# Four small moves in the self-attention stage of a decoder block: sixteen products of ones at the start, one load on another queue, the first snapshot earlier among the exponentials, and a third output tile begun before the last pair

## The chip, the cores and the metric

The kernel runs on one core of a Trainium2 chip. The metric is the time of one execution on the device, in microseconds (us); lower is better. Three executions of the kernel before took 1611.61, 1611.78 and 1612.36 us, so their median is 1611.78 us.

A core has five engines with an instruction stream each: the matrix engine (PE in the profile, with its weight loads as PEld), the vector engine (DVE), the scalar engine (ACT), the general engine (POOL) and the sync engine (SP), which here only issues DMA transfers. They wait for each other through semaphores.

## The reference

Inputs are x (8 batches of 224 rows, 512 columns) and a context (8 of 750 rows, 384 columns), all in 32-bit floats. The block has three parts, each followed by a residual add and a layernorm. Only the first is touched:

```python
x = _rmsnorm(tokens, norm_w)
q = x @ Wq;  k, v = split(x @ Wkv)          # 16 heads of 64
q, k = _head_rmsnorm(q, q_gamma), _head_rmsnorm(k, k_gamma)
sim = tanh(q k^T / 50) * 50 * 64**-0.5
out = softmax(sim) @ v
x = layernorm(tokens + out.reshape(...) @ Wo)
```

After it come a cross-attention against the context (with Wq, Wk, Wv, Wo and a bias) and a feed-forward part with ternary weights and 8-bit activations.

## The kernel before

**Tiling and turns.** The 8·224 = 1792 rows are 14 tiles of 128 rows, and four groups g of two batches (448 rows, `G`). The 16 heads are 8 pairs hp. The self-attention stage runs 32 turns, m = 8g + hp: one head pair of one group each (loop at L758). A turn is a software pipeline over three head pairs: it multiplies the weights of pair m-1 with the values (`self_values`, L632), makes the scores of pair m (`self_scores`, L559), and makes q and k of pair m+2 (`products_qk`, L475). In most turns one tile of v (`project_v`, L539) or one finished tile of the output projection (`self_output`, L661) follows. The order on each engine is the order in which this code is written; no scheduler changes it.

**Scores and exponentials.** `self_scores` issues the score products of both batches u into two PSUM tiles (`sc_a`) and returns a list of eight scalar-engine calls (L585): for u = 0 tanh of 128 rows, tanh of 96 rows, exp of 128 rows, exp of 96 rows, then the same for u = 1. They all have line L282 in the profile (L772 in the last two turns) and write `pr`.

**Seven products instead of eight.** `half_products` (L274) makes q and k of two batches by a Strassen-like scheme: seven half-size products over three PSUM accumulators x_, z_ and w_ (`q_x`, `q_z`, `q_w` at L470; each product is two matmuls of 224 columns, which the profile shows as four instructions). The accumulator x_ is used four times in a row without being cleared. Between two uses the scalar engine takes a snapshot of it: m1 after the first product (L296, tile `qm`), u2 after the second (L304, `qu`), u4 after the third (L312, `qu`). The next product into x_ has to wait until the snapshot is taken. The order of the products is x_, z_, x_ (+s2·t2), w_, x_ (+s1·t1), w_, x_ (+s4·b22).

The eight calls of the exponentials are popped between these instructions by `filling(n)`. Their order on the scalar engine before the change is: three calls, m1, three calls, u2, one call, the copy c22 (L309), one call, u4 (L312), c11 (L315), and later c12 (L328). The snapshots m1 and u2 lie among the exponentials in the same queue, so both the calls ahead of a snapshot and the product that it reads decide when it is taken.

**What else the scalar engine does in a turn.** It squares q and k (L499), which waits for a vector-engine add (L324); it moves v from PSUM to its place (L554), in as many pieces as the tile has runs of rows that may go with one instruction, one to four, of about 0.68 us each; and it squares a tile of x (L371). The eight calls of the next turn stand behind all that.

**Start and end.** `first_loads` (L105) issues the first loads on SP: a tile of transposed x, the norm weights, 128 columns of Wq (`load_cols(0, 0, P)`, L108), three more tiles of transposed x, and so on. `weigh_x` (L393) multiplies a tile by the norm weights on the vector engine, and `block_qk` (L405) makes q of the first pair from it, tile by tile. At the end (L855 to L863) two of the last four tiles get the output products of the first seven pairs, then the values of the last pair are made and scaled on the vector engine (`weigh`, L649), POOL copies the rows that straddle two groups (`oT_joint`, L659), and then the two tiles get their last pair and the other two tiles all eight pairs.

The matmul accumulators of 128 x 512 come from a pool of three (`a_mm`), the score tiles from a pool of two (`a_sc`, which also gives w_), and the tile of the weighted values from a pool of one (`a_ov`).

Of the kernel before, what the change touches and what calls it, by code (L numbers as in the profile page):

```python
# [21 lines left out]
F32 = mybir.dt.float32  # L22
# [17 lines left out]
P = 128  # L40
# [6 lines left out]
NPAIR = HEADS // 2  # L47
# [18 lines left out]
def decoder_block(ctx: ExitStack, tc: tile.TileContext, a: dict, out: bass.AP):  # L66
    nc = tc.nc
# [11 lines left out]
    def load_x(i):  # L79
        nc.sync.dma_start(out=x[i], in_=x_in[i * P : (i + 1) * P, :])  # L80
# [7 lines left out]

    ws = [wpool.tile([P, KD, INNER], F32, tag="w", name=n) for n in ("wq", "wk", "wv")]

    def load_cols(j, c0, c1):

        name, at = (("attn_Wq", 0), ("attn_Wkv", 0), ("attn_Wkv", INNER))[j]
        src = a[name].rearrange("(k p) n -> p k n", p=P)
        nc.sync.dma_start(out=ws[j][:, :, c0:c1], in_=src[:, :, at + c0 : at + c1])

    norm_w = const.tile([P, KD, 1], F32, name="norm_w")
    gam = const.tile([P, 2, NPAIR, 1], F32, name="gam")
# [3 lines left out]
    def load_xT(y, i):  # L102
        nc.sync.dma_start(out=y, in_=xT_in[:, :, i * P : (i + 1) * P])

    def first_loads(xnT):  # L105
        load_xT(xnT[:, :, :P], 0)
        nc.sync.dma_start(out=norm_w[:, :, 0], in_=a["norm_w"])
        load_cols(0, 0, P)  # L108
        for i in range(1, 4):
            load_xT(xnT[:, :, i * P : (i + 1) * P], i)  # L110
        load_cols(1, 0, P)
        load_cols(2, 0, 512)
        for i in range(4):
            load_x(i)
        nc.sync.dma_start(out=gam[:, 0, :, 0], in_=a["q_gamma"])
        nc.sync.dma_start(out=gam[:, 1, :, 0], in_=a["k_gamma"])
        for cols in ((P, 2 * P), (2 * P, INNER)):
            for j in range(2):
                load_cols(j, *cols)
        for i in range(4, NX // 2):  # L120
            load_x(i)
        load_cols(2, 512, INNER)
        for i in range(NX // 2, NX):
            load_x(i)
# [68 lines left out]
    ones = const.tile([P, P], F32, name="ones")  # L193
# [35 lines left out]
    def pieces(i):  # L229

        at = i * P
        while at < (i + 1) * P:
            b = at // S
            n = min((i + 1) * P, (b + 1) * S) - at
            yield b, at - b * S, at - i * P, n
            at += n
# [7 lines left out]
    def key_pieces(i):  # L244

        for b, c, at, n in pieces(i):
            while n:
                kt = c // P  # L250
                row = c % P
                m = min([n, P - row] + [64 if s == 64 else 32 for s in (row, at) if s])
                yield b, kt, row, at, m
                c, at, n = c + m, at + m, n - m
# [16 lines left out]

    def half_products(product, a, b, sums_a, sums_b, dest, parts, acc, third=None, fill=None):  # L274

        def filling(n):  # L280
            for _ in range(n if fill else 0):
                fill.pop(0)()  # L282

        between = bool(fill)
        (a11, a12), (_, a22) = a
        (b11, _), (b21, b22) = b
        s1, s2, s3, s4 = sums_a
        t1, t2, t3, t4n = sums_b
        c11, c12, c21, c22 = (dest(r, c) for r in range(2) for c in range(2))
        m1, u2, u4 = parts  # L290
        x_, z_, w_ = acc
        if third:
            a13, a23, b31, b32, dif = third
        filling(3)
        product(x_, a11, b11, True)
        nc.scalar.copy(m1, x_)  # L296
        filling(3)
        product(z_, a12, b21, True)
        if third:
            product(z_, a13, b31, False)  # L300
        if not between:
            nc.scalar.copy(c11, z_)
        product(x_, s2, t2, False)
        nc.scalar.copy(u2, x_)  # L304
        filling(1)
        product(w_, s3, t3, True)
        if third:
            product(w_, a23, b32, False)
        nc.scalar.copy(c22, w_)  # L309
        filling(1)  # L310
        product(x_, s1, t1, False)
        nc.scalar.copy(u4, x_)  # L312
        if between:
            nc.gpsimd.tensor_tensor(c22, c22, u4, ALU.add)
            nc.scalar.copy(c11, z_)  # L315
            nc.gpsimd.tensor_tensor(c11, c11, m1, ALU.add)
        else:
            nc.gpsimd.tensor_tensor(c11, c11, m1, ALU.add)
            nc.gpsimd.tensor_tensor(c22, c22, u4, ALU.add)
        yield  # L320
        product(w_, a22, t4n, False)
        if third:
            product(w_, a23, dif, False)
        nc.vector.tensor_tensor(c21, w_, u2, ALU.add)  # L324
        product(x_, s4, b22, False)
        if third:
            product(x_, a13, b32, False)
        nc.scalar.copy(c12, x_)  # L328
        yield
# [6 lines left out]
    NG = B // 2  # L336
# [6 lines left out]
    opened = [range(first[g], first[g + 1]) for g in range(NG)]  # L343

    with tc.tile_pool(name="a_sb", bufs=2) as sb, tc.tile_pool(
        name="a_mm", bufs=3, space=PSUM
    ) as ps_mm, tc.tile_pool(name="a_sc", bufs=2, space=PSUM) as ps_sc, tc.tile_pool(
        name="a_ov", bufs=1, space=PSUM
# [119 lines left out]
        def product_qk(mm, c, w, start):  # L468
            for k in range(2):
# [2 lines left out]
                    skip_group_check=True,  # L472
                )

        def products_qk(m, calls):  # L475
            g, hp = divmod(m, NPAIR)
            qk[m] = sb.tile([P, 2, G], F32, name="qk", bufs=3)
            x_, z_ = (ps_mm.tile([P, S], F32, tag="mm", name=f"q_{n}") for n in "xz")
            w_ = ps_sc.tile([P, 2, 512], F32, tag="sc", name="q_w")[:, 0, :S]
            if m < NPAIR + 2:  # L480
                q, k = ([w[:, 2 * kh : 2 * kh + 2, hp * P : (hp + 1) * P] for kh in range(2)]
                    for w in (wq, wk))
                b = (q[0], None), (q[1], k[1])
                t = [work[:, hp % 4, i] for i in range(4)]
            else:
                w7 = stream[:, m % 2]
                b = (w7[:, 0], None), (w7[:, 1], w7[:, 2])
                t = [w7[:, 3 + i] for i in range(4)]
            return half_products(
                product_qk, input_blocks(g), b, [sums_x[:, i] for i in range(4)], t,  # L490
                lambda u, w: qk[m][:, w, u * S : (u + 1) * S],
                [sb.tile([P, S], F32, name=n, bufs=1) for n in ("qm1", "qu2", "qu4")],
                [x_, z_, w_],
                fill=calls,
            )

        def square_qk(m):
# [163 lines left out]
        def self_output(g, i, hp0=0, hp1=NPAIR):  # L661

            if hp0 == 0:
                outs[i] = ps_mm.tile([P, DIM], F32, tag="mm", name="mm_o")
            mm = outs[i]
            at = i * P - g * G
            for hp in range(hp0, hp1):
                o = oT[g * NPAIR + hp].rearrange("p u q -> p (u q)")
                nc.tensor.matmul(  # L669
                    mm,  # L670
                    lhsT=joint[g][:, hp, :] if at < 0 else o[:, at : at + P],
                    rhs=wo[:, hp, :],
                    start=(hp == 0),
                    stop=(hp == NPAIR - 1),
                )
            if hp1 < NPAIR:
                return
            nc.vector.tensor_tensor(x[i], mm, x[i], ALU.add)
            due.append(i)
# [48 lines left out]
            nc.sync.dma_start(out=wq7[:, 3:], in_=sums_xq[:, g])  # L728

        joint, outs, due, scales, ovs = {}, {}, [], [], {}  # L730

        for i in range(4):
            weigh_x(i)
            block_qk(0, 0, (i * P, min((i + 1) * P, G)))
# [19 lines left out]
        for i in opened[0][2:]:  # L754
            project_v(i, 0)

        out_at = [(), (2, 3, 5), (0, 2, 4, 6), (3, 5, 6)]
        for m in range(NS):  # L758
            g, hp = divmod(m, NPAIR)
            ahead = opened[g + 1] if g + 1 < NG else ()  # L760
# [38 lines left out]
            tiles = opened[g + hp // 4] if g + hp // 4 < NG else ()  # L799
# [55 lines left out]
        last = closed[NG - 1]  # L855
# [1 line left out]
            self_output(NG - 1, i, 0, NPAIR - 1)  # L857
        self_values(NS - 1)
        weigh(NS - 1)
        for i in last[:2]:  # L860
            self_output(NG - 1, i, NPAIR - 1)
        for i in last[2:]:
            self_output(NG - 1, i)  # L863

        for f in [layernorm([i]) for i in due]:
# [7 lines left out]
    parts = const.tile([P, 3, NCHUNK], F32, name="w_parts")  # L873
# [56 lines left out]
    with tc.tile_pool(name="c_sb", bufs=1, reuse_waits="tile") as sb, tc.tile_pool(  # L930
        name="c_mm", bufs=7, space=PSUM, reuse_waits="tile"
    ) as ps_mm, tc.tile_pool(
        name="c_nm", bufs=1, space=PSUM, reuse_waits="tile"
# [466 lines left out]
        for t, i0, i1 in ((18, 0, 7), (26, 7, LATE)):  # L1400
            job(t, roots, i0, i1)
            n = t + 1
# [9 lines left out]
        for i in range(NX):  # L1412
            b = ((i + 1) * P - 1) // S
# [9 lines left out]
        for t in range(-1, TURNS):  # L1423
# [19 lines left out]
            fill = []  # L1443
            if t == TURNS - 1:
                fill = [
                    partial(cross_project, i, k, k + 2)
                    for i in done[t] for k in range(0, NPAIR - 2, 2)
                ]
# [52 lines left out]
            if t % (2 * QG) >= 2 * QG - 2 and t > 0 and t + 2 < TURNS:  # L1501
                b = 2 * (t // (2 * QG) + 1) + t % 2
# [13 lines left out]
        last = done[TURNS]  # L1516
# [12 lines left out]
    with tc.tile_pool(name="f_sb", bufs=2, reuse_waits="tile") as sb, tc.tile_pool(  # L1529
        name="f_mm", bufs=6, space=PSUM, reuse_waits="tile"  # L1530
    ) as ps_mm, tc.tile_pool(
        name="f_dn", bufs=2, space=PSUM, reuse_waits="tile"
# [215 lines left out]
```

## Time and profile before

| what | value |
|---|---|
| median of three executions | 1611.78 us |
| the profiled execution: its time, its span | 1611.31 us, 1609.5 us |
| PE busy | 1588.8 us (99% of the span) |
| PEld busy | 1138.0 us (71%) |
| DVE busy | 1326.7 us (82%) |
| ACT busy | 996.8 us (62%) |
| POOL busy | 961.8 us (60%) |
| self-attention | from 0 to about 492 us |

The span is from the first to the last instruction of the program. A busy time counts the stretches in which an engine had an instruction at work; waiting, branching and DMA issuing are not counted. The busy time of PE is that of pipelined matmuls with modelled ends, so neighbours overlap a little: the distance between the starts of two neighbours is the better measure of what a product costs. In a timeline line stand the start in us from the beginning of the span, the length, the engine, the line of the source, what it writes and reads, the shape, and how many instructions were merged; in brackets the idle time of the engine before it and what ended it.

### The profile page before, as it was taken

Reading aid. Unit: us, or ns where it says so; the run is one execution under the profiler, and the core shown is the slowest. Engines: PE = TensorE matmul, PEld = TensorE weight load, DVE = VectorE, ACT = ScalarE, POOL = GpSimd, SP = SyncE. Lnnn points to the kernel's source line nnn. Section 1 sums busy time; section 2 is a strip of 40 time slices with the busy share of each in tenths; the row PEclk is TensorE's granted clock in tenths of the full one; section 3 lists DMA queues with packets and bytes.
Section 4 is the critical chain, followed back from the end, with each engine's and each line's share of the span. In section 5 each row is a group of like instructions: output and inputs, shape, how many; then the busy total and the mean of one; then the engine's idle time right before and its main releaser. Section 6 shows DMA issues by size and latency. Waiting matters only on the chain.

```text
span 1609.5 us, 27132 instructions
## 1 busy us (share of the span) xinstructions
PE 1588.8 (99%) x9668; PEld 1138.0 (71%) x9682; DVE 1326.7 (82%) x2813; ACT 996.8 (62%) x1858; POOL 961.8 (60%) x887
## 2 busy tenths in 40 slices
PE   8999999999999999999999999999999999999998
PEld 5767666667747888876887876788876888764443
DVE  3999897889976798886798886798887898978877
ACT  5667555656525677764667775687764666635663
POOL 5785575666524757685465685457686566752244
PEclk9999999999999999999999999999999999999999
DMA  8115242433204313241122252223240111214343
GB/s 300 47 53 196 81 133 89 138 89 118 82 20 161 104 56 103 65 154 57 60 66 80 78 187 63 72 77 121 78 161 24 34 44 39 75 46 92 66 92 105
DMA packets 143111, 149.14 MB, mean 93 GB/s; under 512 B 41088, under 2 KB 109184, under 8 KB 142592
## 3 DMA queue, kind: packets, MB, share of 16 engines
q1 hardware_dynamic: 142976, 147.40, 30.0%
q8 instruction: 77, 1.26, 0.3%
q14 instruction: 58, 0.48, 0.1%
HBM read 119.85 MB, written 18.87 MB: 86 GB/s over the span
## 4 chain that ended last, share of the span: by engine, by line
PE 85%; DVE 9%; ACT 2%; issue 2%; DMA 1%; POOL 0%; SPq 0%; POOLq 0%; DVEq 0%; ACTq 0%
PE sc_c L1244 9%; PE ov_c L1374 8%; PE v_x L1075 6%; PE mm_co L262 6%; PE mm_f L1547 6%; PE k_x L1069 5%; PE mm_v L544 5%; PE q_x L470 5%; PE v_w L1075 5%; PE k_w L1069 4%; PE mm_o L669 4%; PE mq_x L1082 3%; PE v_z L1075 2%; PE q_w L470 2%; PE sc_a L571 2%; PE ov_a L640 2%
## 5 line engine op out<-in xcount | busy, mean ns | idle before, releaser
L1361 POOL TENSOR_TENSOR csh<-cpT 125x672 f32<-125x672 f32 x128 | 210.0, 1640 | 111.0 <-DVE cpT L1346 94.3
L200 POOL TENSOR_TENSOR nm_i<-nm_q,mhalf 128x28 f32<-128x28 f32 x32 | 157.9, 4935 | 81.8 <-DVE nm_q L519 81.4
L1346 DVE TENSOR_TENSOR cpT<-cpT,mx_b 125x1344 f32<-125x1344 f32 x128 | 192.6, 1545 | 2.8
L1226 ACT COPY cpT<-sc_c 125x448 f32<-125x448 f32 x384 | 173.5, 570 | 17.6 <-PE sc_c L1244 10.6
L1358 ACT ACTIVATE cpT<-cpT 125x1344 f32<-125x1344 f32 x128 | 168.4, 1328 | 11.4 <-DVE cpT L1346 11.2
L1244 PE MATMUL sc_c<-cq,ckT 64*125 64x224 f32 x1536 | 164.2, 359 | 3.4 <-ACT cpT L1226 1.7
L1244 PEld LDWEIGHTS sc_c<-cq,ckT 64*125 64x125 f32 x1536 | 147.7, 183 | 19.1 <-issue 10.3
L1374 PE MATMUL ov_c<-cpT,cv 125*64 125x224 f32 x1536 | 152.9, 355 | 0.2 <-ACT cpT L1358 0.2
L1106 POOL TENSOR_TENSOR cv<-cv,cvmu 125x384 f32<-125x384 f32 x32 | 31.9, 997 | 195.3 <-ACT cv L1105 195.3
L1374 PEld LDWEIGHTS ov_c<-cpT,cv 125*64 125x64 f32 x1536 | 107.6, 137 | 44.6 <-issue 8.8
L544 PE MATMUL mm_v<-wv,xnT 128*128 128x512 f32 x224 | 100.4, 592 | 0.0
L1547 PE MATMUL mm_f<-ternary,xqT 128*128 128x512 bf16 x435 | 98.0, 379 | 1.5 <-DVE h L1557 0.8
L262 PE MATMUL mm_co<-xattn_Wo,coT 128*128 128x512 f32 x224 | 98.5, 593 | 0.0
L1230 DVE TENSOR_TENSOR xw<-sc_c,cpT 125x448 f32<-125x448 f32 x64 | 39.7, 620 | 67.6 <-PE sc_c L1244 59.0
L282 ACT ACTIVATE pr<-sc_a 128x448 f32<-128x448 f32 x120 | 57.9, 535 | 60.4 <-PE sc_a L571 60.2
L1362 POOL TENSOR_TENSOR csm<-csh 125x224 f32<-125x224 f32 x128 | 85.0, 664 | 10.0
L1363 POOL TENSOR_TENSOR csm<-csm,csh 125x224 f32<-125x224 f32 x128 | 84.5, 660 | 10.0
L595 DVE TRANSPOSE_TENSOR_REDUCE sm_q<-pr 128x28 f32<-128x896 f32 x64 | 70.7, 1104 | 19.3 <-ACT pr L282 18.9
L1254 ACT COPY ov_s<-ov_c 128x448 f32<-128x448 f32 x31 | 16.5, 531 | 110.7 <-PE ov_c L1374 110.7
L669 PE MATMUL mm_o<-attn_Wo,oT 128*128 128x512 f32 x192 | 84.3, 593 | 0.0
L1547 PEld LDWEIGHTS <-xqT 128*128 128x128 bf16 x448 | 43.8, 98 | 54.2 <-issue 1.7
L554 ACT ACTIVATE v<-mm_v,rms_rs 32x512 f32<-32x512 f32 (+2 forms) x80 | 54.4, 680 | 36.7 <-PE mm_v L544 35.9
(239 smaller groups left out, 3967.1 us busy)
## 6 DMA issues: line engine op xcount, KB each, us to landing
w_slot<-qk_sums SPq DMA_DIRECT2D x22, 512.0 KB, 3.6
xw<-w_sums SPq DMA_DIRECT2D x32, 320.0 KB, 2.9
xwq<-xq_sums SPq DMA_DIRECT2D x16, 512.0 KB, 4.2
w_stage<-w_gateT SPq DMA_DIRECT2D x16, 512.0 KB, 5.4
w_stage<-w_upT SPq DMA_DIRECT2D x16, 512.0 KB, 4.9
w_stage<-w_downT SPq DMA_DIRECT2D x16, 512.0 KB, 4.5
tern<-w_t SPq DMA_DIRECT2D x24, 256.0 KB, 2.7
ternary<-tern SPq DMA_DIRECT2D x3, 2048.0 KB, 7.8
```

The source lines that it names most:

```text
L200: nc.gpsimd.tensor_tensor(y, v, mhalf.to_broadcast([P, v.shape[-1]]), ALU.pow)
L262: nc.tensor.matmul(mm, lhsT=oT[:, k, c : c + P], rhs=w[:, k, :], start=(k == 0), stop=(k == NPAIR - 1),)
L544: nc.tensor.matmul(mm, lhsT=xnT[:, k, at : at + P], rhs=wv[:, k, c * 512 : (c + 1) * 512], start=(k == 0), stop=(k == KD - 1),)
L669: nc.tensor.matmul(mm, lhsT=joint[g][:, hp, :] if at < 0 else o[:, at : at + P], rhs=wo[:, hp, :], start=(hp == 0), stop=(hp == NPAIR - 1),)
L1075: nc.tensor.matmul(mm[:, t, :], lhsT=c[:, t * CT : (t + 1) * CT], rhs=w, start=start and t == 0, stop=True, skip_group_check=True,)
L1226: nc.scalar.copy(pT[:, j, 2 * c2 : 2 * c2 + 2, :], banks[c2][j])
L1244: nc.tensor.matmul(sc[j][:, i, :], lhsT=kT[h0 : h0 + DH, w, ct * CT : (ct + 1) * CT], rhs=cq[h0 : h0 + DH, t % 2, w], start=True, stop=True,)
L1346: nc.vector.tensor_tensor(pT[:, j], pT[:, j], nm[:CT, j] .rearrange("p (o q) -> p o q", o=1) .to_broadcast([CT, NCT, S]), ALU.add,)
L1358: nc.scalar.activation(pT[:, j], pT[:, j], AF.Exp)
L1361: nc.gpsimd.tensor_tensor(half, pT[:, j, 0:3], pT[:, j, 3:6], ALU.add)
L1374: nc.tensor.matmul(ov[h0 : h0 + DH, w, :], lhsT=v[:, ct, hq * DH : (hq + 1) * DH], rhs=pTs[w][:, j, ct, :], start=(ct == 0), stop=(ct == N ...
L1547: nc.tensor.matmul(mm, lhsT=xqTs[i][:, k, :], rhs=w[:, k, cols], start=(k == 0), stop=(k == KD - 1),)
```

## The change

Four edits, all in the self-attention stage:

1. Ahead of the first `weigh_x`, PE gets 16 matmuls of a 128 x 128 tile of ones with itself, into the tile `ov_a`. Nothing reads the result, and the tile's next user overwrites it. They wait only for POOL's memset of the ones (L194).
2. The first 128 columns of Wq are issued from the scalar engine's queue, where they are the first instruction after the entry barrier, ahead of the load of the activation tables. They were third on SP's queue.
3. `half_products` pops `ahead` calls before m1 and 6 - `ahead` between m1 and u2, in place of three and three. `products_qk` passes 0 in the turns that `crowded` names and 2 in the others. `crowded(m)` holds in turn 0, and where the v tile of turn m-1 has four or more pieces and that turn had no output tile. Worked out, it holds in turns 0, 3, 6, 7, 10, 15, 22, 26 and 27; the products are made in turns 0 to 29, so 21 turns have `ahead=2`.
4. At the end the third of the four last tiles gets its first seven pairs after the last values and their scaling are issued, and before the last pair of the first two tiles.

```diff
-    def load_cols(j, c0, c1):
+    def load_cols(j, c0, c1, queue=nc.sync):
...
-        nc.sync.dma_start(out=ws[j][:, :, c0:c1], in_=src[:, :, at + c0 : at + c1])
+        queue.dma_start(out=ws[j][:, :, c0:c1], in_=src[:, :, at + c0 : at + c1])
...
-        load_cols(0, 0, P)
+        load_cols(0, 0, P, nc.scalar)
...
-        filling(3)
+        filling(ahead)
         product(x_, a11, b11, True)
         nc.scalar.copy(m1, x_)
-        filling(3)
+        filling(6 - ahead)
         product(z_, a12, b21, True)
...
+        def crowded(m):
+
+            g, hp = divmod(m - 1, NPAIR)
+            if m == 0:
+                return True
+            tiles = opened[g + hp // 4] if g + hp // 4 < NG else ()
+            n = len(list(key_pieces(tiles[hp % 4]))) if hp % 4 < len(tiles) else 0
+            return n >= 4 and hp not in out_at[g]
...
+                ahead=0 if crowded(m - 2) else 2,
...
+        warm = ps_ov.tile([P, 2, 256], F32, name="ov_a")
+        for i in range(16):
+            nc.tensor.matmul(
+                warm[:, i % 2, :P], lhsT=ones, rhs=ones, start=True, stop=True
+            )
...
         self_values(NS - 1)
         weigh(NS - 1)
-        for i in last[:2]:
+        self_output(NG - 1, last[2], 0, NPAIR - 1)
+        for i in last[:3]:
             self_output(NG - 1, i, NPAIR - 1)
-        for i in last[2:]:
+        for i in last[3:]:
             self_output(NG - 1, i)
```

In the call of `crowded`, m - 2 is the turn in which the products are made, since `products_qk` is called with m + 2.

More of the change, by code (lines that the diff above doesn't have):

```diff
@@ L269, in project_out, with half_products @@
         return mm
-    def half_products(product, a, b, sums_a, sums_b, dest, parts, acc, third=None, fill=None):
+    def half_products(product, a, b, sums_a, sums_b, dest, parts, acc, third=None, fill=None, ahead=0):
         def filling(n):
@@ L730, in decoder_block @@
         joint, outs, due, scales, ovs = {}, {}, [], [], {}
+        out_at = [(), (2, 3, 5), (0, 2, 4, 6), (3, 5, 6)]
+        warm = ps_ov.tile([P, 2, 256], F32, name="ov_a")
[3 more added lines that the diff above has]
+            )
         for i in range(4):
@@ L755, in decoder_block @@
             project_v(i, 0)
-        out_at = [(), (2, 3, 5), (0, 2, 4, 6), (3, 5, 6)]
         for m in range(NS):
```

## The prediction

> **What bounds the kernel now.** I read the page's busy times and the shares of the chain first. They say that PE holds the end: what is taken off PE's own sequence, or put into it as idle time, moves the end by as much.
>
> ```profile
> PE 1588.8 (99%) x9668; PEld 1138.0 (71%) x9682; DVE 1326.7 (82%) x2813; ACT 996.8 (62%) x1858; POOL 961.8 (60%) x887
> PE 85%; DVE 9%; ACT 2%; issue 2%; DMA 1%; POOL 0%; SPq 0%; POOLq 0%; DVEq 0%; ACTq 0%
> ```
>
> Next the waits of PE alone over the first 480 us (PE is at work almost without a break from 5.2 us on). Three causes are all there is, and each of the four edits aims at one of them:
>
> ```profile
> PE mm_qk L416 <- DMA wq<-attn_Wq: 5.2, 1, 5.2
> PE q_x L470 <- ACT qm L296: 2.9, 5, 1.5
> PE mm_o L669 <- POOL oT_joint L659: 1.0, 1, 1.0
> ```
>
> The 2.9 us on snapshot m1 fall in five turns (0, 3, 7, 9 and 10). In the other 25 turns with products PE does not wait at all, so there the third edit has nothing to win. What it may lose is seen in the timeline of a turn without waits, turn 1:
>
> ```profile
> 47.67 1.78 PE L571 MATMUL sc_a<-qk 64*128 64x224 f32 x16
> 48.75 0.97 ACT L282 ACTIVATE pr<-sc_a 128x448 f32<-128x448 f32 x2 [1.34 <-PE sc_a L571]
> 49.61 0.57 ACT L282 ACTIVATE pr<-pr 128x448 f32<-128x448 f32 x1
> 50.25 0.92 PE L470 MATMUL q_z<-xnT,wq 128*128 128x224 f32 x4
> 50.45 0.35 ACT L296 COPY qm<-q_x 128x224 f32<-128x224 f32 x1 [0.27 <-PE q_x L470]
> 50.69 0.58 ACT L282 ACTIVATE pr<-pr 96x448 f32<-96x448 f32 x1
> 51.01 0.93 PE L470 MATMUL q_x<-x_sums,w_room 128*128 128x224 f32 x4
> 51.17 0.96 ACT L282 ACTIVATE pr<-sc_a 128x448 f32<-128x448 f32 x2
> 51.77 0.92 PE L470 MATMUL q_w<-x_sums,w_room 128*128 128x224 f32 x4
> 52.02 0.34 ACT L304 COPY qu<-q_x 128x224 f32<-128x224 f32 x1
> 52.53 0.92 PE L470 MATMUL q_x<-x_sums,w_room 128*128 128x224 f32 x4
> ```
>
> See three things. (a) ACT waits 0.27 us for the first x_ product and takes m1 0.20 after that product ends (50.25): m1 is held by PE, not by the exponentials. (b) From m1 (50.45) to u2 (52.02) ACT runs without a break: 0.24 for the copy, 0.48 for one exp, 0.85 for two tanh. (c) u2 ends at 52.36; a snapshot's end releases PE 0.14 later (turn 0: m1 ends 38.47, PE starts 38.61), so the third x_ product could start at 52.50, and it starts at 52.53, when w_ is done. The slack is 0.03 us. I worked out the same difference for all 30 turns from their timelines: 0.02 to 0.03 in 28, -0.04 (none) in two.
>
> **The third edit, the snapshot.** The calls of the exponentials keep their lengths and their number; only what stands between m1 and u2 changes.
>
> *Turns with two calls ahead (21).* Now two exps and two tanh stand between m1 and u2: 0.24 + 2 x 0.465 + 0.86 = 2.03 where it was 1.57. (0.465 is one exp behind another: in the last two turns the exps start 0.94 before the next call.) In a turn like turn 1, m1 cannot come earlier, since it waits for PE. So u2 starts 0.46 later, and PE starts the third x_ product late by 0.46 less the slack: 0.44. Twenty turns are of this kind: 20 x 0.44 = 8.8. In turn 9, where ACT comes 0.94 late to the scores, m1 moves up from 148.44 to 147.97 and removes that turn's wait of 0.40, but u2 lands where it was (149.99, now 150.00): +0.04. The wait goes from m1 to u2.
>
> *Crowded turns (9).* All six first calls stand behind m1, and m1 behind the x_ product. From the start of the scores to the end of x_ are 2.57 us in every turn, and m1 follows at 2.77. Turn 6 shows when ACT could have begun:
>
> ```profile
> 109.82 1.78 PE L571 MATMUL sc_a<-qk 64*128 64x224 f32 x16
> 111.03 0.97 ACT L282 ACTIVATE pr<-sc_a 128x448 f32<-128x448 f32 x2
> ```
>
> That is 1.21 after the scores, against 1.07 in turn 1: late by 0.14 only. Behind m1, ACT then sits idle from 1.21 to 2.77, 1.56 us, with six calls to do before u2: 0.24 + 1.00 (two tanh) + 0.93 (two exp) + 0.86 (two tanh) = 3.03. u2 starts at 2.77 + 3.03 = 5.80 and PE goes on 0.48 later at 6.28; it did at 114.67 - 109.82 = 4.85. Loss 1.43. Turns 6, 15, 22, 26, 27 (tanh at 1.21 or 1.22 in all) give 5 x 1.44 = 7.2. Turns 0, 3 and 10, where PE waited 0.65, 0.28 and 0.18 for m1 and ACT starts at 1.96 to 2.20, give by the same steps +0.54, +0.79 and +0.85. Only turn 7, where ACT starts 3.05 after the scores, has nothing to lose: -0.03.
>
> Sum: 8.8 + 0.04 + 7.2 + 2.18 - 0.03 = 18.2. Nothing covers it: PE is the engine that holds the end, and between turns it has no other idle time to give back. One part comes back: turn 7 is late because DVE's adds lag (ACT's square waits 3.95 us for L324 there), and a PE that has lost some 4 us by then finds DVE less far behind. Turn 7 then ends like turn 6, 6.28 after its scores instead of 6.60, and turns 8 to 10 gain a little: 0.5 off. The exps end later by 0.46 to 1.6, and DVE's sums, queued in front of the scaling of the next pair's q and k, wait for them; that scaling ended at 55.04 for scores at 60.00, which leaves 4 us. Term: **+17.7**. Low end 15 (slack and exp each read 0.05 in favour, and all DVE-made waits of 2.1 us gone), high end 21 (DVE or POOL late by another 0.1 a turn).
>
> **The first and second edits, the start.** PE's first product waits for the Wq columns until 5.23. It then runs at half pace, and the pace changes at about 10.7:
>
> ```profile
> 5.20:7.30 2.10, 2.07 (x9) 1.99 (x10) 0.72 (x2) 0.00 (x0) 0.00 (x0) 1.00 1.12 305
> 7.30:10.70 3.40, 3.40 (x17) 3.40 (x18) 1.50 (x3) 0.00 (x0) 0.00 (x0) 1.00 1.07 365
> 492.02 1.91 PE L1036 MATMUL tr_x<-ident,x 128*128 128x128 f32 x16
> ```
>
> The columns are the stretch, its length, then PE's busy time and instructions. Seventeen 128-column instructions took 3.40 us, 0.20 each; later sixteen took 1.91, and 512 columns start 0.43 apart, so 0.107 for 128. The clock row shows 1.00 throughout and does not tell of this; the pace does. It changed 5.5 us after the first product.
>
> After the change the ones are ready at 1.09 (memset 0.89 + 0.20), so 32 instructions of ones run from 1.15. With the same 5.5 us, 27 are done slowly by 6.65 and 5 quickly by 7.2. Then q of the first pair (24 instructions of 128 columns, 8 of 64) takes 24 x 0.107 + 8 x 0.054 = 3.0 and ends at 10.2 instead of 11.56: -1.4. Ends: a change after 3.4 us (the shortest for which the rows leave room, since 17 slow instructions fill 3.4) gives 9.0, -2.5; a change at 10.7 as before, with the ones slow to 7.6, 15 slow instructions after them and 9 x 0.107 + 8 x 0.054 quick ones, gives 12.1, +0.5. I take the middle one, since its 5.5 us is the one that this trace shows. The Wq load moves past norm_w on SP (0.43 us of issue, and SP's later loads move up by it) and lands about when the first tile does; but its data are wanted at 7.2 now, so the second edit is worth nothing by itself. It costs ACT one issue ahead of a table load that is done at 2.0, with ACT's first work at 11.76. The next data are in time: Wk landed at 8.98, Wv at 11.69, needed at 10.2 and 13.3. PE has no wait from there to turn 0, so the gain stays: **-1.4**.
>
> The Trainium skill, "TensorE: Matmul & The Clock Gate", Part 1 ("What's actually happening"), says that the clock is released after a busy window of about 3.4 us that runs freely. The trace agrees with 5.5 us (a part window and a whole one); by the page alone the start would gain between 0.7 and 2.4, an estimate. "DMA: Bandwidth & Descriptors", "Rules for kernel authors", says that spreading loads over issuing engines only saves issue time. That speaks against the second edit; by it the load's share is 0.43 at most, against nothing in my sum.
>
> **The fourth edit, the end.** The last pair's values end at 475.44 and the first output product after them waits for the vector engine and POOL:
>
> ```profile
> 475.49 0.62 DVE L653 TENSOR_TENSOR oT<-ov_a,rc_a 128x448 f32<-128x448 f32 x1 [4.59 <-PE ov_a L640]
> 476.18 0.24 POOL L659 COPY oT_joint<-oT 128x64 f32<-128x64 f32 x1 [8.46 <-DVE oT L653]
> 476.47 1.12 PE L669 MATMUL mm_o<-attn_Wo,oT_joint 128*128 128x512 f32 x2 [1.02 <-POOL oT_joint L659]
> ```
>
> The fourteen instructions of the third tile (6.0 us) go into that gap, with the same number in all: **-1.0**. What is late next: the fourth tile needs the accumulator of the first, whose add (0.69) is done 0.9 us after its last product, while PE has 1.7 us of the second and third tile's last pairs to do. The adds of the first two tiles come 6 us later, and nothing reads them before the layernorms, which stood behind the fourth tile's add anyway.
>
> **Sum.** 17.7 - 1.4 - 1.0 = +15.3. The profiled execution took 1611.31 (span 1609.5), 0.47 under the median of 1611.78. 1611.31 + 15.3 = 1626.6; on the median 1627.1. I predict 1627.
>
> **The rivals.**
> A, the other side: m1's waits vanish and u2 costs nothing, because u2 can be late by the added call without holding PE. Price: -2.9 - 1.4 - 1.0, so 1606.5. It decides if the slack of u2 is over 0.46 us in the plain turns and 1.5 in the crowded ones; measured are 0.02 to 0.03. Chance 0.05, for an order of releases that I misread.
> B, crowded turns cost less: if ACT comes later to them than the trace shows, because DVE lags more behind the later exps, then a first m1 costs nothing there, as in turn 7. Then 8.8 + 1 - 2.4 = +7.4, 1619. Against it: DVE gains time with each stall of PE. Chance 0.10.
> C, DVE becomes a second bound: its sums wait for the exps in all turns; 0.3 us more in each of 30 turns is 9 us, 1636. For it: DVE is busy 385 of 439 us of the stage. Chance 0.10.
>
> **How the numbers follow.** My forecast has 0.75. Its own range, from the ends of the terms (15 - 2.5 - 1.0, and 21 + 0.5 - 0.8), is 1623 to 1632. With B's upper half and C's lower tail in it, 8 in 10 lie between 1621 and 1632. A measurement of this kernel tells 0.2% (3.2 us) from no change. All cases but A are slower by more; with a little for a cancelling mixture: faster 0.05, same 0.02, slower 0.93.
>
> **What would show it.** The waits of PE should list the third x_ product behind the `qu` snapshot of L304 in some 28 turns, with 0.4 us in the plain ones and about 1.4 in the crowded ones, 17 to 18 us in all; waits on `qm` gone; ACT idle before `qm` by 0.7 us in plain turns and 1.6 in crowded ones; the q of the first pair done at about 10 us; no wait on `oT_joint`. I am wrong if `qu` shows no waits, or if ACT starts a crowded turn's m1 later than 2.8 us after its scores.

## The result

The changed kernel takes 1629.92 us (median of four executions, 1628.33 to 1630.88) against 1612.07 us for the kernel before, measured beside it. The ratio is 1.0109, with a 95% interval of 1.0094 to 1.0124: 18 us slower. The forecast was 1627 us, with 8 chances in 10 between 1621 and 1632.

Where it went, from the two profiled executions (spans 1609.5 and 1628.2 us; the bounds are the starts of PE's first scores, of the scores of turn 30, of the last turn's scores, and of the first transposes of the next stage):

| stretch | before, us | after, us | difference | forecast |
|---|---|---|---|---|
| start to the first scores | 34.46 | 33.48 | -0.98 | -1.4 |
| turns 0 to 29 | 414.87 | 434.01 | +19.14 | +17.7 |
| last turn's scores to the next stage | 32.25 | 31.15 | -1.10 | -1.0 |
| everything after self-attention | 1117.48 | 1119.14 | +1.66 | 0 |

The engines' busy times (page of the kernel after) show PE with 13 us more, though its work has grown by the ones only (about 6 us): the rest is the stretch at half clock below, and waiting that the modelled ends of the matmuls cover. In the shares of the chain, ACT has gone from 2% to 5%.

```profile
PE 1601.7 (98%) x9714; PEld 1141.4 (70%) x9714; DVE 1328.2 (82%) x2813; ACT 996.9 (61%) x1858; POOL 961.2 (59%) x887
PE 87%; ACT 5%; DVE 5%; issue 1%; DMA 1%; POOL 0%; POOLq 0%; SPq 0%; DVEq 0%
```

The waits of PE over the first 500 us of the kernel after have one big line in place of three. (A wait counts here from the modelled end of the product before, so each entry is 0.16 us or more short of what the starts show.)

```profile
PE q_x L470 <- ACT qu L304: 14.7, 30, 1.1
PE ov_a L745 <- POOL ones L194: 1.2, 1, 1.2
```

The snapshot m1 no longer holds PE anywhere; the snapshot u2 (tile `qu`, L304) holds it in all 30 turns. Turn 1 of the kernel after, in the timeline, with the waits in brackets:

```profile
47.26 1.78 PE L581 MATMUL sc_a<-qk 64*128 64x224 f32 x16
48.34 0.97 ACT L282 ACTIVATE pr<-sc_a 128x448 f32<-128x448 f32 x2 [1.34 <-PE sc_a L581]
49.84 0.92 PE L470 MATMUL q_z<-xnT,wq 128*128 128x224 f32 x4
50.04 0.35 ACT L296 COPY qm<-q_x 128x224 f32<-128x224 f32 x1 [0.73 <-PE q_x L470]
50.28 1.04 ACT L282 ACTIVATE pr<-pr 128x448 f32<-128x448 f32 x2
51.23 0.96 ACT L282 ACTIVATE pr<-sc_a 128x448 f32<-128x448 f32 x2
51.36 0.92 PE L470 MATMUL q_w<-x_sums,w_room 128*128 128x224 f32 x4
52.08 0.34 ACT L304 COPY qu<-q_x 128x224 f32<-128x224 f32 x1
52.47 0.68 PEld L470 LDWEIGHTS q_x<-x_sums,w_room 128*128 128x128 f32 x4 [0.54 <-ACT qu L304]
52.47 1.02 PE L470 MATMUL q_x<-x_sums,w_room 128*128 128x224 f32 x4 [0.19 <-ACT qu L304]
```

m1 comes where it came before, 2.78 us after the start of the scores, because the x_ product is not done earlier. ACT now idles 0.73 us for it, and then has two exps and two tanh to do before u2 instead of one and two. u2 is taken 2.04 us after m1 (1.57 before), and the third x_ product starts 0.35 after the w_ product could have let it. The turn is 0.46 us longer. The other 0.11 is inside that product: its second instruction starts 0.29 after the first, where the distance was 0.19. In the kernel before, its weights were loaded while the w_ product still ran:

```profile
52.41 0.69 PEld L470 LDWEIGHTS q_x<-x_sums,w_room 128*128 128x128 f32 x4
```

That load began 0.05 after the end of u2 (52.36), and the product 0.12 after the load. Now the load too begins 0.05 after u2 (52.42), and no other product hides it. In a crowded turn (6) the gap is larger:

```profile
112.20 1.78 PE L581 MATMUL sc_a<-qk 64*128 64x224 f32 x16
114.97 0.35 ACT L296 COPY qm<-q_x 128x224 f32<-128x224 f32 x1 [1.58 <-PE q_x L470]
115.22 0.97 ACT L282 ACTIVATE pr<-sc_a 128x448 f32<-128x448 f32 x2
118.01 0.34 ACT L304 COPY qu<-q_x 128x224 f32<-128x224 f32 x1
118.40 1.02 PE L470 MATMUL q_x<-x_sums,w_room 128*128 128x224 f32 x4 [1.12 <-ACT qu L304]
```

ACT stands idle for 1.58 us with the scores ready, since m1 is first in its queue; the six calls follow, and PE goes on 6.20 us after the scores where it was 4.85. This turn is 1.46 us longer, 1.35 at the start of that product and 0.11 inside it.

The end of self-attention in the kernel after shows the gap of 1.02 us filled: the third tile's fourteen products follow the values, and the first tile's last pair goes on without a wait.

```profile
491.86 1.74 PE L650 MATMUL ov_a<-pr,v 128*64 128x224 f32 x16
493.53 6.28 PE L679 MATMUL mm_o<-attn_Wo,oT 128*128 128x512 f32 x14
499.64 1.02 PE L679 MATMUL mm_o<-attn_Wo,oT_joint 128*128 128x512 f32 x2
```

The last 1.66 us are put down to chance and not to the change: the code behind self-attention is the same in all kernels below, and their profiled executions took 1117.48 to 1121.11 us for it. Most of the 1.66 us lies in one stretch of 3.4 us, far behind self-attention, in which PE was granted half the clock in this execution. The columns are stretch, length, busy time and instructions of PE, PEld, DVE, ACT and POOL, granted clock, DMA:

```profile
872.80:876.20 3.40, 3.40 (x19) 2.67 (x17) 2.45 (x6) 3.19 (x8) 0.00 (x0) 0.51 0.02 5
```

The products concerned show it: the second half of a score step (24 instructions), and the product after it.

```profile
871.78 4.84 PE L1260 MATMUL sc_c<-cq,ckT 64*125 64x224 f32 x24 [1.61 <-ACT ov_s L1270]
876.55 0.92 PE L1091 MATMUL v_x<-xw,ctx_even 128*125 128x128 f32 x6
```

The same in the kernel before, at the full clock and with a pause of 0.23 us:

```profile
854.23 1.50 PE L1244 MATMUL sc_c<-cq,ckT 64*125 64x224 f32 x10 [1.61 <-ACT ov_s L1254]
855.96 1.89 PE L1244 MATMUL sc_c<-cq,ckT 64*125 64x224 f32 x14 [0.23 <-ACT cpT L1226]
857.78 0.92 PE L1075 MATMUL v_x<-xw,ctx_even 128*125 128x128 f32 x6
```

From the first start to the last these are 4.77 us against 3.55, so the stretch cost 1.22 us. Another 0.49 us had been lost by then, between 509 and 872 us; its cause is open.

### The profile page after: what moved, and what is told of

The parts are those of the page before. It is cut to its first block, busy times and chain, and to the rows that moved or that the text cites. A ratio compares the mean times of both kernels' runs of the same rounds, so it can differ in the third digit from the quotient of the medians.

```text
span 1628.2 us, 27214 instructions
## 1 busy us (share of the span) xinstructions
PE 1601.7 (98%) x9714; PEld 1141.4 (70%) x9714; DVE 1328.2 (82%) x2813; ACT 996.9 (61%) x1858; POOL 961.2 (59%) x887
## 4 chain that ended last, share of the span: by engine, by line
PE 87%; ACT 5%; DVE 5%; issue 1%; DMA 1%; POOL 0%; POOLq 0%; SPq 0%; DVEq 0%
PE sc_c L1260 9%; PE ov_c L1390 8%; PE v_x L1091 6%; PE mm_o L679 6%; PE mm_co L262 6%; PE mm_v L554 6%; PE mm_f L1563 6%; PE k_x L1085 5%; PE q_x L470 5%; PE v_w L1091 5%; PE k_w L1085 4%; ACT pr L282 4%; PE sc_a L581 3%; PE ov_a L650 3%; PE mq_x L1098 3%; PE v_z L1091 2%
## 5 line engine op out<-in xcount | busy, mean ns | idle before, releaser
L554 PE MATMUL mm_v<-wv,xnT 128*128 128x512 f32 x224 | 100.4, 592 | 0.0
```

The lines of the kernel that those rows point to most:

```text
L554: nc.tensor.matmul(mm, lhsT=xnT[:, k, at : at + P], rhs=wv[:, k, c * 512 : (c + 1) * 512], start=(k == 0), stop=(k == KD - 1),)
```

## The experiments

Theory U: what costs is the number of scalar-engine calls between m1 and u2, because the third x_ product waits for u2, whose slack was 0.03 us. Rivals: S, the edits at the start and the end, or an interplay, make part of the loss; D, the exps end later, and the vector engine, whose sums wait for them, holds up the next turns; B, the crowded turns are not dearer than the others. All kernels start from the kernel before, except where a diff is said to be against another. For short, a turn's order is written as four counts: calls ahead of m1, between m1 and u2, between u2 and c22, between c22 and u4; what is left of the eight runs after the copies. Before it was (3, 3, 1, 1), after the change (2, 4, 1, 1), and (0, 6, 1, 1) in crowded turns. Where the order is changed, `half_products` takes the four counts as an argument `n`, with (3, 3, 1, 1) where nothing else is said; the diffs show only the line that sets it. "Loop" is the stretch of turns 0 to 29, 414.87 us before. A "plain" turn is one of the twenty that had no wait for m1 and are not crowded.

Five kernels have four or more executions. The other six (two calls ahead, the two counts, the early m1 with three calls, and the two of the start) have one each, and thirteen executions of the kernel before lie between 1611.07 and 1613.37 us. The loop tells more: with the order unchanged it took 414.87 to 414.92 us in four kernels.

### The snapshot edit alone

```diff
+                n=(0, 6, 1, 1) if m - 2 in (0, 3, 6, 7, 10, 15, 22, 26, 27) else (2, 4, 1, 1),
```

> The third edit alone on the kernel before: 0 calls ahead of m1 in the nine crowded turns, 2 in the others, 6 or 4 between m1 and u2. Theory U (what counts is the number of calls between m1 and u2, and the third x_ product waits for u2): the loop of turns gets 19 us longer, as in the changed kernel, so 1612 + 19 = 1631, and the waits of PE are all on the snapshot of L304. Rival S (the edits at start and end, or an interplay of the four, make a part of the loss): 1622 to 1627.

Measured: 1630.72 us (ratio 1.012, 1.0107 to 1.0134). Its loop is 434.01 us, the same to the hundredth as that of the changed kernel, turn by turn. The wait of PE on u2 is the same line, and the two waits that the other edits take away are there:

```profile
PE q_x L470 <- ACT qu L304: 14.7, 30, 1.1
PE mm_qk L416 <- DMA wq<-attn_Wq: 5.1, 1, 5.1
PE mm_o L670 <- POOL oT_joint L660: 1.0, 1, 1.0
```

The whole loss is the third edit's. S falls.

### The other three edits without it

```diff
-        filling(ahead)
+        filling(3)
...
-        filling(6 - ahead)
+        filling(3)
```

This is against the changed kernel.

> The changed kernel with its third edit undone: ones, load on the other queue and third tile stay. Theory U: start -1.0, end -1.1, so 1612 - 2 = 1610, the m1 waits of the turns 0, 3, 7, 9 and 10 back. Rival S: the three edits cost something together, 1612 to 1615.

Measured: 1609.92 us, ratio 0.999 (0.9981 to 1.0). The loop is 414.87 us again. The first scores start at 33.19 us (34.46 before) and the end takes 31.15 (32.25), so the two gains of 1.3 and 1.1 us are there. The interval of the whole time just reaches 1.0.

### Two calls ahead in every turn

```diff
+                n=(2, 4, 1, 1),
```

> The kernel before with 2 calls ahead of m1 and 4 between m1 and u2 in all 30 turns, no turn treated as crowded. Theory U: each added call between the snapshots costs one exp less the slack, 0.46 to 0.59 a turn, in the 25 turns without an m1 wait, and about nothing in the five late ones: the loop gets 12 to 13 us longer, about 1624 to 1625. Rival B (crowded turns cost no more than the others when m1 goes first, and the loss in the changed kernel comes from elsewhere): no better than the changed kernel's loop, 1629 to 1631.

Measured: 1624.64 us; loop 426.75, +11.88. The crowded turns 6, 15, 22, 26 and 27 cost 0.58 or 0.59 each, where they cost 1.46 with none ahead; the turns 0, 3, 9 and 10 cost -0.10 to 0.01, and turn 7 gained 0.97. B falls: going first with m1 costs 0.87 us more in a turn whose exponentials could have started. (In turn 6 of the changed kernel the scalar engine stood idle for 1.58 us.)

### One call more, one call less between the snapshots

The counts are (2, 5, 1, 0) in all turns of the first kernel and (3, 2, 1, 1) in all turns of the second, where one call is left for the end.

```diff
+                n=(2, 5, 1, 0),
```

```diff
+                n=(3, 2, 1, 1),
```

> Two calls ahead of m1 in all 30 turns, five between m1 and u2 instead of four, none between c22 and u4. Theory U: each turn without an m1 wait of its own loses one exp more than with four calls (0.47 on top of 0.46 to 0.59), and the five late turns lose 0.47 against their loss there: the loop of turns is 26 to 27 us longer than before and 14 longer than with four, 1638 to 1640. Rival D (it is the early m1 or the later end of the exps that costs, not the count): no more than with four calls, 1624 to 1626.

> Three calls ahead of m1 as before the change, but only two between m1 and u2; the one left over runs after the copies. Theory U: u2 is then ready 0.45 early and PE is held by its own products, so the plain turns gain no more than their slack was short, 0.0 to 0.03: the loop stays at 414.9 within 0.5 us, 1611 to 1612. If calls between the snapshots cost in proportion, without a point from which they begin to count, it would gain 12 us.

Measured: 1638.5 us with five between them and 1611.29 us with two. The loops are 440.42 and 414.86 us. What a plain turn costs over the kernel before: two calls 0.00, three calls nothing (that is the kernel before), four calls 0.46 (0.59 in some), five calls 0.92 or 0.93 (1.05 in those). That is a bend at the order before the change: below it nothing is gained, above it each call costs about its own length (0.47). The wait of PE with five calls:

```profile
PE q_x L470 <- ACT qu L304: 21.4, 30, 0.8
```

### The early m1 kept, three calls between

The counts are (2, 3, 1, 1), and (0, 3, 1, 1) in the crowded turns; the calls left over run after the copies. Start and end are those of the kernel before.

```diff
+                n=(0, 3, 1, 1) if m - 2 in (0, 3, 6, 7, 10, 15, 22, 26, 27) else (2, 3, 1, 1),
```

> The third edit's early m1 kept (0 ahead in the nine crowded turns, 2 in the others), but only three calls between m1 and u2, as before the change; the calls left over (three or one) run after the copies. The exps end as late as in the changed kernel or later. Theory U: the waits on u2 shrink to 0.0 to 0.15 a turn, the m1 waits of five turns are gone: 1609 to 1613. Rival D (later exps make the vector engine's sums and the next turns late): the loop stays 10 us or more above that of before, 1622 to 1632.

Measured: 1611.12 us, loop 414.43. The exps of the crowded turns end later than in the changed kernel, and the loss is gone: at most 0.03 in fourteen of the plain turns, 0.13 to 0.16 in the other six (those that cost 0.59 with four calls) and in the crowded turns 6, 15, 22, 26 and 27. D falls as the cause of the loss. But the late exps are not free: at the end of turn 7 a new wait shows.

```profile
PE sc_a L572 <- DVE qk L535: 0.8, 1, 0.8
```

### Another order in the five late turns

The turns 0, 3, 7, 9 and 10, where PE did wait for m1, get the counts (0, 2, 1, 1); the others keep theirs.

```diff
+                n=(0, 2, 1, 1) if m - 2 in (0, 3, 7, 9, 10) else (3, 3, 1, 1),
```

> The kernel before, with another order in the five turns where PE waited for m1 (0, 3, 7, 9, 10): no call ahead of m1, only the two tanh between m1 and u2, one call after u2, one after c22, the last four after the copies. The other turns keep 3, 3, 1, 1. Theory U: u2 can be taken right behind the second x_ product there, so the waits of 2.9 us vanish without coming back on u2: -3 to -4 us, 1608 to 1609. Rival D (the exps that end later hold up the vector engine's sums, and through them the next turns): no gain or a loss, 1612 to 1616.

Measured: 1609.87 us, ratio 0.9991 (0.9982 to 1.0); loop 413.26, -1.61, less than half of what I expected. The turns 0, 3, 9 and 10 gained 0.81, 0.43, 0.50 and 0.44: their waits for m1 (0.65, 0.28, 0.24 and 0.18 in the profile before) and 0.15 to 0.26 more. Turn 7 gained 0.26 instead of 1.5, and the turns 5 and 6 lost 0.57 and 0.28. The vector engine's timeline and PE's waits in this kernel point to why. The sums in turn 3 waited 1.44 us for the late exp, in a stretch (72 to 123 us) in which the vector engine is busy 47.46 of 51 us (48.58 before), so it has little time to catch up. In the turns 5 and 6 ACT comes late to m1 (its square, ahead of them, waits 2.77 and 2.49 us for the vector engine's add, where that wait was 1.1 us or less before), and at the end of turn 7 the scores wait for the scaled q and k:

```profile
76.78 1.11 DVE L596 TRANSPOSE_TENSOR_REDUCE sm_q<-pr 128x28 f32<-128x896 f32 x1 [1.44 <-ACT pr L282]
```

```profile
PE sc_a L572 <- DVE qk L535: 0.8, 1, 0.8
PE q_x L470 <- ACT qm L296: 0.6, 2, 0.3
```

So D is right here, where the vector engine has no slack, though not for the loss of the change.

### The start: ones alone, load alone

```diff
+        for i in range(16):
+            nc.tensor.matmul(warm[:, i % 2, :P], lhsT=ones, rhs=ones, start=True, stop=True)
```

> The kernel before with the sixteen products of ones alone. If the ones set the start: first q done at about 10.6 as in the changed kernel, 1.0 before that of the kernel before, 1611 us; the load on SP lets the norm weights land at 3.8, but PE is busy with ones until 7. If the load's queue matters as well, first q is done later than 10.6.

```diff
...
-        load_cols(0, 0, P)
+        load_cols(0, 0, P, nc.scalar)
```

> The kernel before with the first Wq columns issued from the scalar engine's queue alone. In the changed kernel the norm weights landed at 5.28 where they had landed at 3.84, and the first weighed tile began at 5.38 where it had begun at 3.94. If the queue does that by itself, PE's first product starts at about 6.1, 0.9 later than before, and the first q ends up to 0.5 later: 1612 to 1613. If the load is free, the first product starts at 5.1 to 5.2 and nothing changes.

Measured: 1611.44 us with the ones alone, 1613.47 us with the load alone (1611.88 for the kernel before beside them). With the ones, q of the first pair is done at 10.33 us (11.56 before) and the first scores start 1.23 earlier. The time shows less of it, because PE in this execution also waits 1.1 us for the scalar engine near 508 us, where the kernel before waits 0.2. With the load alone PE's first product starts at 6.20 us instead of 5.23, and the trace names the norm weights, which are now under way together with the first columns of Wq:

```profile
5.45 1.39 DVE L396 TENSOR_TENSOR xnT<-xnT,norm_w 128x512 f32<-128x512 f32 x2 [4.57 <-DMA norm_w<-norm_w]
6.20 5.50 PE L416 MATMUL mm_qk<-xnT,wq 128*128 128x128 f32 x32 [6.20 <-DVE xnT L396]
```

They land at 5.35 us, where they landed at 3.84. The second edit costs about 1 us at the first product; the first q still ends at 11.54, since the pace changed 3.6 us after the first product here and 5.5 in the kernel before. By itself it is a loss that this chance covered. In the changed kernel the ones cover the delay, as PE is busy with them until 7.05. (The longer time of 1613.47 us does not come from the start: the first scores start at 34.44 us, 34.46 before. A stretch at half clock stands in this execution too, at 856 us.)

### A version that beats both

Ten products of ones, the load left on SP, the third tile begun at the end, and the order of the late turns.

> The order of the kernel late_turns, with ten matmuls of ones at the start, the Wq load left on SP, and the third tile begun at the end. Theory U: -3.5 from the turns, -1.1 from the end, and at the start -1.8 (ones done at 5.4 in place of 7.05, then held by the fourth weighed tile at 8.8, first q done at 9.8 against 11.56): 1612 - 6.4 = 1605.6. Rival D: 1609 or more.

Measured: 1607.34 us, ratio 0.9977 (0.9968 to 0.9986). The first scores start at 33.01 (-1.45), the loop is 413.27 (-1.60), the end 31.15 (-1.10). The start gave 0.4 less than I had worked out: the fewer ones end at 5.48, and q is done at 10.10.

> As the kernel best (ten ones, the load on SP, the third tile begun at the end), but with the early snapshot and short distance to u2 only in the turns 7, 9 and 10; 0 and 3 are as before the change. In late_turns the vector engine waited 1.44 us for an exp of turn 3, in the stretch where it is busy 95% of the time, and PE lost 0.57 and 0.28 again in the turns 5 and 6. If that wait gave back the gain of the turns 0 and 3, turn 7 now gains 1.5 and 9 and 10 gain 0.9: loop -2.4, 0.8 us better than best, 1606.5. If the turns 5 to 7 are late in any case, the loop gains 1.2 to 1.6 and the time is 1607 to 1608.

Against the kernel above:

```diff
-                n=(0, 2, 1, 1) if m - 2 in (0, 3, 7, 9, 10) else (3, 3, 1, 1),
+                n=(0, 2, 1, 1) if m - 2 in (7, 9, 10) else (3, 3, 1, 1),
```

Measured: 1607.34 us, ratio 0.9974 (0.9964 to 0.9984): no better. The turns 5 and 6 lost nothing this time, so that loss came with the other order of the turns 0 and 3. But turn 7 gained 0.49 only, the loop 1.43. So it is not the wait in turn 3 alone: the vector engine makes the turns around 7 late in any case, and PE's wait of 0.8 us for it at the end of turn 7 is there again. What a lighter vector engine in the turns 2 to 7 would give was not tried.

## Why the prediction was right, and where its sizes were off

*The third edit, turns with two calls ahead.* Right in mechanism, a little low in size. Forecast were 0.44 for each of twenty turns; fourteen cost 0.46, six (4, 14, 16, 20, 23, 25) cost 0.59. Sum 10.0 where I had 8.8. In these six the first exp comes 0.13 later than in the others: in the kernel before 1.00 after the first tanh instead of 0.86, where the wait for m1 hid it, and in the kernel after 0.37 after m1 instead of 0.24. The term that I mis-sized is this 0.24, which I took for all twenty turns, though in the crowded turns I had read the longer distance (1.00 for two tanh). The traces show a pattern: in the kernel before the exp is late in thirteen turns, and these are just the turns in which a copy of v (L554) was the scalar engine's last work before the exponentials. In the other seventeen it was a square or a small copy. What brings it about was not tested.

The 0.44 was also put together differently from what came. The third x_ product starts only 0.35 late, and the other 0.11 is inside it (turn 1 above). I had taken 0.14 from a snapshot's end to PE's next product from an m1; at u2 it is 0.05, but the load of the weights, which had run under the product before, waits for u2 as well. u2 comes 0.47 later and the turn is 0.46 longer, so the slack was nearer to 0.01 than to 0.03. The list of waits shows 14.7 us on `qu` where I had named 17 to 18, since it counts from the modelled ends.

Turn 9 gave -0.10 for a forecast of +0.04. I had left the scalar engine late there; it came on time, with the first tanh 1.07 after the scores (2.02 before). The wait of 0.40 that I named for that turn is 0.24 in the profile; the sum does not use it.

*Crowded turns.* Forecast 1.44 each, measured 1.46 in all five. Here two small errors cancel: PE goes on 6.20 us after the scores where I had 6.28, and the product is 0.11 longer. For 0.54, 0.79 and 0.85 in turns 0, 3 and 10 came 0.57, 0.82 and 0.82. Turn 7 gained 0.28, as the correction for the vector engine's lag had it (6.28 instead of 6.60 us, so 0.32). Of the 0.5 that I took off for that, about 0.4 came back, in the turns 7, 9 and 10.

*The start.* Forecast -1.4, measured -0.98. The pace changed sooner than I took it to, 4.7 us after the first product instead of 5.5, which ended the ones 0.15 earlier. But the eight 64-column instructions do not take half as long as those of 128: the trace has them 0.11 apart like the others, which is 0.4 us that I had not counted, and 0.111 instead of 0.107 for the other 24 makes another 0.1. How much of this size is chance is said at the end. I had called the second edit "worth nothing by itself". The Trainium skill, "DMA: Bandwidth & Descriptors", "Rules for kernel authors", has a saving of issue time as all that such a spread can bring, which would be 0.43 us at most here. The traces show a harm: the norm weights land 1.4 us later (5.28 instead of 3.84), which the ones hid.

*The end.* Forecast -1.0, measured -1.10 in every kernel that has it.

*What was not in the sum:* 1.66 us behind self-attention in the profiled execution, 1.22 of it in the stretch at half clock. The three stretches of self-attention alone give +17.1 where the forecast has +15.3. With the start and the turns both above their forecast and the 1.66 us on top, the result lies in the upper half of the range.

*The rivals.* A (snapshot costs nothing) was off: every turn's slack was as small as the trace had shown. B (cheap crowded turns) was off: the scalar engine was ready in them, 1.58 us before m1 in turn 6. C (the vector engine as a second bound) did not come with the change: the waits of the scalar engine's square for the vector engine's add fell from 28.4 us in twelve turns to 15.1 in seven. But it is what limits the improved orders.

## What to carry to other kernels

Where one queue holds several releases, look at the slack of all of them before moving work between them: the snapshot that the waits named was late in five turns, while the next one in the same queue had 0.03 us of slack or less in all thirty, and each call moved ahead of it cost nearly its full length (0.46 us of 0.47 in a plain turn). An instruction put first in such a queue before its input is there holds the calls behind it, though they could run (1.58 us of idle time in turn 6).

## What the runs showed of the hardware beyond that

The half-clock stretch is one of chance. Of the thirteen profiled executions seven have none between self-attention and the last microseconds of the program, and that part took 1117.48 to 1118.81 us. Six have one of 3.4 us, and it took 1118.62 to 1121.11 us. Measured against the kernel before, the products around the stretch took 1.1 to 1.6 us longer. (The two ranges overlap because other things vary too: in the execution of 1118.81 us and in that of 1121.11 PE also waits 1.1 and 1.3 us near 508 us, which the others do not.) In five of the six the stretch begins 0.7 to 1.8 us behind the end of the 1.6 us in which PE waits for ACT (L1254 before the change); in one it begins at 510 us, 1.6 us behind a wait of 1.33 us. The wait of 1.6 us also stands in all the executions without a stretch there. So a wait of PE of less than 2 us was followed by a further loss of more than 1 us, in some executions and not in others. That the wait brings it about is argued from where the stretches lie; whether products of ones in that wait would prevent them was not tried.

The change of pace at the start came 2.9 to 5.8 us after PE's first product in these executions, so that the first q without ones was done anywhere from 10.83 to 11.83 us for the same instructions. With sixteen ones it was done at 10.28 to 10.57. So the gain of 0.98 us at the start holds for the pair compared above; other pairs give 0.26 to 1.55. The Trainium skill, "TensorE: Matmul & The Clock Gate", Part 1 ("What's actually happening"), has the change after one busy window of about 3.4 us that runs freely; the spread of 2.9 us fits that, but the shortest case, 2.9 us after the first product, is shorter than a whole window.
